# Late constants, larger first pieces, key rotations on GpSimd and reordered seams in a two-layer decoder block

## The chip, the cores and the metric

The kernel runs on one core of a Trainium2 chip. The metric is the device time of one execution in microseconds; of several executions the median is given. A core has a matrix engine (TensorE, "PE" in the profile, with its weight loads as "PEld"), a vector engine (VectorE, "DVE"), a scalar engine (ScalarE, "ACT"), GpSimd ("POOL") and SyncE ("SP"), which here issues most transfers. Each engine works through its own instructions in order and waits on semaphores for the others. Operands lie in SBUF; matmul results lie in PSUM banks.

## What is computed

The input is `x` of 2 x 512 x 1024 and a context `ctx` of 2 x 1024 x 1024, in float32. Four blocks follow each other, each added to `x`:

```python
x = x + matmul(fake_quant(layernorm(x)), fake_quant(ctx))       # quantized product, "layer 0"
x = x + linear_with_routed_lora(layernorm(x))                   # 1024 x 1024, 8 experts of rank 16
x = x + attention(layernorm(x), ctx, ctx, wq, wk, wv, wo)       # 32 query heads, 8 key/value heads, rotary
x = x + linear(layernorm(x)) + gated_lora(layernorm(x))         # 1024 x 1024, the best of 4 experts of rank 8
```

Keys and values depend on the context alone; rotary embedding multiplies keys and queries by a cosine and adds their swapped halves times a sine. The softmax subtracts the row maximum, and its denominators divide the result.

## The kernel before

Nearly every large product is done as a 2x2 block product with seven block products instead of eight (the Strassen-Winograd form). `left_steps` and `right_steps` (L242, L256) form the four extra operands of each side with additions. `seven` (L270) issues the products in the order 1, 2, 6, 7, 5, 4, 3 and hands the four result blocks to `emit`. After product 1 ScalarE copies the accumulator out of PSUM (L284); after the others VectorE adds it (L288, L291, L293, L297, L300). A product of four f32 matmuls of 128x128 by 128x512 (L355, each two instructions of some 0.43 us start to start) takes 3.43 us. `seven_onto` (L304, with the copy at L320 and the addition at L328) does the same onto rows of `x`. Results go to four PSUM buffers of the tag `b` and two of `wide`; SBUF buffers come from the rings `u2`, `u4` and `u8`.

PE's instructions run in the order in which they are written, throughout. In the first stage the orders of DVE and ACT are also written by hand, in the attention loop those of DVE, ACT and POOL. Elsewhere a scheduler orders these engines and the issue queues.

The stages, with their place in the trace: the keys of batch 0 in two halves of weights (q = 0 and 1, held in the list `first`), to about 110 us; the values of batch 0, to 230; the keys and values of batch 1, to 460; the linear block with its LoRA, then the queries, to about 930; attention, to 2300; the last block, to 2448. While PE works at keys and values, the quantized product of layer 0 is woven in (`weave`, L343: one stretch of the side work after every second product).

The first stage loads its weights (`wk_raw`) on SP and its context (`ctx_raw`) mostly on ACT's queue, the first block of each in four pieces. Eight small constants (the quantizer's scales and zero points, router and expert biases, the router matrix, the gate matrix) are loaded on POOL's queue, and DVE works out five values from them ahead of everything. `keys` (L482) rotates each block with `rope` (L208): two swapped-half copies on ACT (L216, L217), then a cosine multiplication (L219), a sine multiplication (L222) and an addition (L223) on DVE. Then SP stores the block (L494). The value weights are loaded by `quad_weights` (L364, loads at L370) after the weave of keys(0, 1), and DVE forms their sums.

`queries` (L668) does the same as the keys for the 32 query heads, eight at a time for the two batches. The last pair (q = 7) runs inside the first attention iterations, with sines on POOL.

`attention` (L856) is a loop over 64 heads (2 batches x 32), with three heads in flight: scores of head n+2 (L768, evicted by DVE with the mask at L782), exponentials of head n+1 (DVE subtracts the maximum at L814, ACT does the exponential at L817, POOL and DVE sum at L820 to L825) and the weighted values of head n (L831). Row maxima and denominators are turned into rows with transposes (L732), a reduction (L734) and two small DMAs through DRAM (`to_row` with L741, `from_row` with L747). Each finished head is divided by its denominators on POOL (`normalize`, L842). Iterations n = -2 and -1 fill the loop; the table `extra` says how many query products are issued within each of the first iterations. Work for the last block hangs on some iterations by `hooks`; `gated` (L956) makes the gate in stretches: matmuls (L967), copies on ACT (L975), then transposes (L981) and a chain of small DVE operations (L982 to L996) that choose the expert.

Of the kernel before, what the change touches and what calls it, by code (L numbers as in the profile page):

```python
# [39 lines left out]
def decoder_kernel(  # L40
# [75 lines left out]
    qp = {}  # L116
    for name, ap in qparams.items():
        t = const.tile([P, 1], F32, name=f"qp_{name}")
        nc.gpsimd.dma_start(t, ap.partition_broadcast(P))
        qp[name] = t  # L120
    for side in ("x1", "x2"):
        t = const.tile([P, 1], F32, name=f"qp_inv_{side}")
        nc.vector.reciprocal(t, qp[f"{side}_scale"])
        qp[f"{side}_inv"] = t

    c_x1 = const.tile([P, 1], F32, name="c_x1")
    c_x2 = const.tile([P, 1], F32, name="c_x2")
    for c_t, side in ((c_x1, "x1"), (c_x2, "x2")):
        nc.vector.tensor_scalar(c_t, qp[f"{side}_zp"], -1.0, QMID, ALU.mult, ALU.add)
    kc2 = const.tile([P, 1], F32, name="kc2")  # L130
    nc.vector.tensor_scalar_mul(kc2, c_x2, float(D))
    s12 = const.tile([P, 1], F32, name="s12")
    nc.vector.tensor_tensor(s12, qp["x1_scale"], qp["x2_scale"], ALU.mult)
    ident_b = const.tile([P, P], BF16, name="ident_b")
# [3 lines left out]
    rb_t = const.tile([P, E0], F32, name="rb_t")  # L138
    nc.gpsimd.dma_start(rb_t, rb0.partition_broadcast(P))
    eb_t = const.tile([P, E1], F32, name="eb_t")  # L140
    nc.gpsimd.dma_start(eb_t, ebias.partition_broadcast(P))
    r0_t = const.tile([P, NC, E0], F32, name="r0_t")
    nc.gpsimd.dma_start(r0_t, r0T.rearrange("(c p) e -> p c e", p=P))
    NGA = E1 + E1 * R1
    ga_t = const.tile([P, NC, NGA], F32, name="ga_t")
    nc.gpsimd.dma_start(ga_t, gaT.rearrange("(c p) e -> p c e", p=P))
    cos_t = [const.tile([P, HALF], F32, name="cos_t"), None]
# [59 lines left out]

    def rope(dst, acc, half, scale):  # L208

        for _ in rope_steps(dst, acc, half, scale, nc.vector):  # L210
            pass
# [57 lines left out]

    def seven(product, emit):  # L270

        banks = {}
        for i in (1, 2, 6, 7, 5, 4, 3):
            first = {2: 1, 4: 7, 3: 5}.get(i, i)
            if i == first:
                banks[i] = ps_b()
            acc = banks[first]  # L280
            product(i, acc, i == first)
            if i == 1:
                u, c22, c21 = u2([P, HALF]), None, None
                nc.scalar.copy(u, acc)  # L284
            elif i == 2:
                emit(0, 0, acc)
            elif i == 6:
                nc.vector.tensor_tensor(u, u, acc, ALU.add)  # L288
            elif i == 7:
                c22 = u2([P, HALF])  # L290
                nc.vector.tensor_tensor(c22, u, acc, ALU.add)  # L291
            elif i == 5:
                nc.vector.tensor_tensor(c22, c22, acc, ALU.add)  # L293
                emit(1, 1, c22)
            elif i == 4:
                c21 = u2([P, HALF])
                nc.vector.tensor_tensor(c21, u, acc, ALU.add)  # L297
                emit(1, 0, c21)
            else:
                nc.vector.tensor_tensor(u, u, acc, ALU.add)  # L300
                emit(0, 1, u)
            yield
# [61 lines left out]
    def quad_weights(dram, q):  # L364

        raw = []
        for mh in range(2):
            for ch in range(2):
                w = u4([P, 4, 256])
                nc.sync.dma_start(w, dram[q, mh, ch])  # L370
                raw.append(w)
        return quad_sums(raw)

# [107 lines left out]

    def keys(b, q, ctx_ops, w):  # L482
        def group(m):
# [7 lines left out]
            def emit(i, j, src):  # L491
                dst = u2([P, HALF]) if (i, j) == (0, 0) else src
                rope(dst, src, j, 1.0)
                nc.sync.dma_start(kT_d[b][4 * q + 2 * i + m][:, ts(j, HALF)], dst)  # L494

            return seven(product, emit)

# [169 lines left out]

    def queries(q, h_ops, w, later=None):  # L668

        def head(m):  # L670
# [7 lines left out]
            def finish(i, j, src):  # L678
                dst = u2([P, HALF]) if (i, j) == (0, 0) else src
                eng = nc.vector if later is None else nc.gpsimd  # L680
                yield from rope_steps(dst, src, 0, ATT_SCALE, eng)
# [174 lines left out]
    def attention(extra):  # L856
# [28 lines left out]
        for n in range(-2, total + GRP + 1):  # L885
# [33 lines left out]
            if n > GRP and gg + 1 < B * NKV:  # L919
                for i in {2: (1, 6, 2), 3: (7, 5, 4, 3)}.get(k, ()):  # L920
                    w_ops[i] = output_operand((gg + 1) % NKV, i)
            for _ in range(extra.pop(n, 0)):
                for _ in range(2):
                    next(tree, None)
                next(extra["products"])
            if n == GRP:
                w_ops = {i: output_operand(0, i) for i in (1, 6, 2, 7, 5, 4, 3)}
# [3 lines left out]

            if mid:
                mid.place_maximum()
# [5 lines left out]
            if old:  # L939
                old.attend(0)  # L940
            if mid:
                mid.exponential(0)
            if old:
                old.den = from_row(old.den)
                if new:
                    new.turn_maximum()
            if mid:
                mid.exponential(1)
            if new:
# [92 lines left out]

    for c in range(4):
        cs = slice(c, c + 1)
        nc.sync.dma_start(wk_raw[0][0][:, cs, :], wk[0, 0, 0][:, cs, :])
# [15 lines left out]
    for ch in range(2):  # L1061
        load_weight(1, 1, ch)


    ctx_ops = [ctx_raw[0], ctx_raw[2]] + [None] * 5
    w = [wk_raw[q][0:2] + [None] * 5 for q in range(2)]
    first = [keys(0, q, ctx_ops, w[q]) for q in range(2)]

# [7 lines left out]
    with tc.manual_schedule(engines={mybir.EngineType.DVE, mybir.EngineType.Activation}):  # L1076
        rights = right_steps(nc.vector, *ctx_raw, lambda: u8([P, 4, HALF]))
        lefts = left_steps(nc.vector, *wk_raw[0], lambda: u4([P, 4, 256]))
        advance(rights, 2)
        advance(lefts, 2)  # L1080
        for g in first[0]:
            next(g)
# [15 lines left out]
        load_rows(0, nc.scalar)  # L1098

    side = layer_0()  # L1100
    for b in range(B):
# [5 lines left out]
        for i, stage in enumerate((keys, keys, values, values)):  # L1107
# [6 lines left out]
            if (b, i) == (0, 1):  # L1114
                main = chain(*first[1])
            else:
                main = pair(*stage(b, i % 2, ctx_ops, w))
            weave(main, side, 2)
            if i < 3:
                w = quad_weights((wk, wv)[(i + 1) // 2], (i + 1) % 2)  # L1120
            if i == 1 and b == 1:
# [42 lines left out]
    h_ops = [hb[0][0], hb[0][1]] + [None] * 5  # L1164
    early = [head for q in range(2) for head in queries(q, h_ops, w[q])]
    for _ in range(2):
# [8 lines left out]
    for q in range(NH // 4):  # L1175
        heads = (
            early[2 * q : 2 * q + 2]
            if q < 2
            else queries(q, h_ops, w, later if q == NH // 4 - 1 else None)
        )  # L1180
        main = chain(*heads) if q < 2 else pair(*heads)
        for g in ((0,), (1,), (2,), (3,), (4,), (5,), (6, 7), ())[q]:
            output_sums(g)
        if q < NH // 4 - 1:
            for _ in main:
                pass
            if q > 0:
# [3 lines left out]

    extra = {-2: 3, -1: 3, 0: 2, 1: 2, 2: 2, 3: 1, 4: 1}
    steps = attention({**extra, "products": main, "later": later})
# [39 lines left out]
    for i in range(2):  # L1233
# [10 lines left out]
    ]  # L1244
    hooks[(62, 1)] = [lambda: advance(last["gates"], 3)]
    hooks[(62, 2)] = [
        lambda: fetch_weight(7, 0, 1),
        lambda: fetch_weight(3, 1, 1),
# [146 lines left out]
```

## Time and profile before

| | us |
|---|---|
| median of 3 runs | 2449.82 (2448.38 to 2452.53) |
| the profiled execution | 2450.07 |
| its span in the profile | 2448.3 |
| PE busy | 2412.5 |
| DVE busy | 1841.1 |
| ACT busy | 530.8 |
| POOL busy | 1031.3 |

The mean granted clock of TensorE was 0.999. By stage, from the trace (busy us of each engine):

| stretch | PE | DVE | ACT | POOL |
|---|---|---|---|---|
| 4 to 110, keys of batch 0 | 102.31 | 74.13 | 21.43 | 2.93 |
| 114 to 230, values of batch 0 | 113.88 | 77.96 | 13.59 | 0.00 |
| 230 to 350, keys of batch 1 | 118.03 | 94.72 | 27.41 | 11.36 |
| 350 to 460, values of batch 1 | 110.00 | 51.61 | 13.46 | 4.02 |
| 930 to 980, seam to attention | 44.99 | 34.41 | 10.37 | 12.12 |
| 980 to 2300, attention | 1312.23 | 1148.65 | 341.71 | 935.85 |
| 2300 to 2448, last block | 143.72 | 71.61 | 9.67 | 40.48 |

A row of the profile reads: start, duration, engine, line of the kernel, operation, output<-input with shapes, count, and in brackets the idle time before it with what ended that wait. A row of waits gives the total, the count and the longest. Matmuls are pipelined, so small sums of busy time say less than the starts do. The loads of the first 35 us moved 9.63 MB.

### The profile page before, as it was taken

How to read it: one execution, taken by the hardware profiler on the slowest of the kernel's cores; microseconds unless marked ns; L12 is line 12 of the kernel's file. 1: busy time of each engine (PE TensorE's matmuls, PEld its weight loads, DVE VectorE, ACT ScalarE, POOL GpSimd, SP SyncE). 2: the span in 40 equal slices, each digit the busy share in tenths (PEclk: the TensorE clock that was granted, in tenths of full speed). 3: DMA queues.
4: the chain of work that ended last, by engine and by line, in shares of the span. 5: the costliest groups of instructions: out<-in, count | busy, mean ns of one | idle time of the engine just before them, and what ended most of it. 6: DMA issues, size and time to landing. Idle time of an engine off the chain costs nothing.

```text
span 2448.3 us, 19583 instructions
## 1 busy us (share of the span) xinstructions
PE 2412.5 (99%) x6792; PEld 1195.8 (49%) x6800; DVE 1841.1 (75%) x1994; ACT 530.8 (22%) x623; POOL 1031.3 (42%) x550
## 2 busy tenths in 40 slices
PE   8999999999999999999999999999999999999999
PEld 3477458654444443444444444444444444444444
DVE  4949774345876556898888888888898998888653
ACT  1210221011222222322222222222222222222210
POOL 0000010210000001677676767667776767677621
PEclk9999999999999999999999999999999999999999
DMA  5537133013796221244323323442433343233501
GB/s 182 181 105 273 69 134 108 26 60 116 274 330 216 78 91 56 77 156 111 81 83 107 114 65 90 142 145 79 125 116 79 94 125 112 66 90 108 172 9 60
DMA packets 149010, 288.01 MB, mean 118 GB/s; under 512 B 29424, under 2 KB 47360, under 8 KB 146608
## 3 DMA queue, kind: packets, MB, share of 16 engines
q1 hardware_dynamic: 108080, 244.35, 29.9%
q10 hardware_dynamic: 40400, 41.70, 6.9%
q8 instruction: 54, 0.88, 0.2%
q0 software_dynamic: 432, 0.71, 0.1%
q14 instruction: 44, 0.36, 0.1%
HBM read 223.54 MB, written 63.18 MB: 117 GB/s over the span
## 4 chain that ended last, share of the span: by engine, by line
PE 60%; DVE 6%; POOL 2%; issue 1%; DMA 1%; ACT 1%; ACTq 0%; SPq 0%; DVEq 0%; POOLq 0%
PE b L355 26%; PE wide L768 16%; PE b L831 15%; PE wide L732 2%; DVE u L814 2%; DMA u<-in_wo_dram 1%; DVE u L782 1%; POOL u L823 0%; POOL u L824 0%; DVE small L734 0%; DVE u L792 0%; DVE u L794 0%; ACT u L817 0%; POOL u L825 0%; DVE u L328 0%
## 5 line engine op out<-in xcount | busy, mean ns | idle before, releaser
L355 PE MATMUL b<-u,u 128*128 128x512 f32 (+1 forms) x3616 | 1394.2, 542 | 21.3 <-DMA u<-in_ctxT_in_dram 7.6
L355 PEld LDWEIGHTS b<-u,u 128*128 128x128 f32 x3616 | 684.6, 191 | 695.9 <-issue 612.8
L768 PE MATMUL wide<-u,u 128*128 128x512 f32 x1024 | 454.8, 595 | 7.3 <-DVE u L782 6.4
L831 PE MATMUL b<-u,u 128*128 128x512 f32 x1024 | 460.3, 592 | 0.0
L782 DVE TENSOR_TENSOR u<-wide,u 128x1024 f32<-128x1024 f32 x256 | 312.8, 1224 | 130.3 <-PE wide L768 129.9
L817 ACT ACTIVATE u<-u 128x2048 f32<-128x2048 f32 x128 | 244.7, 1912 | 655.8 <-DVE u L814 593.9
L768 PEld LDWEIGHTS wide<-u,u 128*128 128x128 f32 x1024 | 193.4, 190 | 257.3 <-issue 177.9
L814 DVE TENSOR_TENSOR u<-u,b 128x2048 f32<-128x2048 f32 x128 | 290.2, 2268 | 0.0
L820 POOL TENSOR_TENSOR u<-u 128x1024 f32<-128x1024 f32 x64 | 151.5, 2367 | 317.5 <-ACT u L817 310.1
L831 PEld LDWEIGHTS b<-u,u 128*128 128x128 f32 x1024 | 186.2, 192 | 184.6 <-issue 184.6
L310 POOL TENSOR_TENSOR u<-u,u 128x512 f32<-128x512 f32 x120 | 188.5, 1597 | 175.4 <-DVE u L322 153.2
L328 DVE TENSOR_TENSOR u<-u,b 128x512 f32<-128x512 f32 x200 | 135.8, 680 | 126.0 <-PE b L355 125.9
L222 POOL TENSOR_TENSOR u<-u,sin_t 128x512 f32<-128x512 f32 x8 | 11.6, 1456 | 402.7 <-ACT u L217 402.7
L823 POOL TENSOR_TENSOR u<-u,u 128x1024 f32<-128x1024 f32 x64 | 150.7, 2354 | 36.4 <-ACT u L817 36.0
L824 POOL TENSOR_TENSOR u<-u,u 128x1024 f32<-128x1024 f32 x64 | 150.8, 2356 | 5.0
L842 POOL TENSOR_TENSOR u<-u,u 128x512 f32<-128x512 f32 x64 | 119.9, 1873 | 10.0 <-DMA u<-row 10.0
L216 ACT ACTIVATE u<-u 64x512 f32<-64x512 f32 x72 | 45.2, 628 | 356.3 <-DVE u L293 177.6
L790 DVE TENSOR_TENSOR u<-u 128x1024 f32<-128x1024 f32 x64 | 115.8, 1810 | 0.0
L732 PEld LDWEIGHTS wide<-ident,u 128*128 128x128 f32 x512 | 79.6, 203 | 63.9 <-issue 55.0
L612 POOL TENSOR_TENSOR u<-u,u 128x1024 f32<-128x1024 f32 x8 | 20.2, 2529 | 214.9 <-DVE u L168 111.6
L792 DVE TENSOR_TENSOR u<-u,u 128x1024 f32<-128x1024 f32 x64 | 105.4, 1646 | 0.2
L825 POOL TENSOR_TENSOR u<-u 128x512 f32<-128x512 f32 x64 | 101.0, 1578 | 5.0
(135 smaller groups left out, 1614.3 us busy)
## 6 DMA issues: line engine op xcount, KB each, us to landing
u<-row ACTq DMA_DIRECT2D x128, 256.0 KB, 3.7
u<-wo SPq DMA_DIRECT2D x64, 512.0 KB, 4.0
u<-in_wo_dram SPq DMA_DIRECT2D x48, 512.0 KB, 4.5
u<-in_wq_dram SPq DMA_DIRECT2D x32, 512.0 KB, 4.2
q<-u SPq DMA_DIRECT2D x64, 256.0 KB, 2.4
u<-in_wo_dram SPq DMA_DIRECT2D x16, 1024.0 KB, 8.2
wo<-u SPq DMA_DIRECT2D x32, 512.0 KB, 4.2
u<-q SPq DMA_DIRECT2D x64, 256.0 KB, 4.2
```

Source lines behind the costliest of these rows:

```text
L310: nc.gpsimd.tensor_tensor(c, c, what, ALU.add)
L328: nc.vector.tensor_tensor(c, c, acc, ALU.add)
L355: nc.tensor.matmul(acc, lhsT, rhs, start=start and k == 0, stop=k == len(pairs) - 1, skip_group_check=True,)
L732: nc.tensor.transpose(tr[:, t, :], src[:, t, :], ident)
L768: nc.tensor.matmul(sc[:, ts(n, HALF)], self.kT[:, ts(2 * j + n, P)], self.qT, start=True, stop=True,)
L782: nc.vector.tensor_tensor(self.e[j // 2][:, js, :], sc.rearrange("p (k q) -> p k q", k=2), mask[j], ALU.add)
L814: nc.vector.tensor_tensor(e, e, self.nmf.unsqueeze(1).to_broadcast([P, 4, S]), ALU.add)
L817: nc.scalar.activation(e, e, AF.Exp)
L820: nc.gpsimd.tensor_tensor(d, e[:, 0:2, :], e[:, 2:4, :], ALU.add)
L823: nc.gpsimd.tensor_tensor(d, d, e[:, 0:2, :], ALU.add)
L824: nc.gpsimd.tensor_tensor(d, d, e[:, 2:4, :], ALU.add)
L831: nc.tensor.matmul(self.acc, self.v[:, k, :], self.e[j][:, k % 4, :], start=(k == 0), stop=(k == NKT - 1),)
```

## The change

Six places are edited.

1. The eight constants are loaded on SP after all other loads of the first stage, and the five values that DVE makes of them are formed after that stage's products in the program's text. The first weight and context blocks come in three pieces, the third of double size. Twenty matmuls of bf16 ones are issued first, into a buffer of the first product. The first product of the first two groups is issued piece by piece, each piece to both groups, and `seven` takes it as `begun`.
2. The value weights' loads are issued before the weave of keys(0, 1); only their sums follow it.
3. `keys` takes an engine for the sine multiplication and the addition, and its queue for the store. The first call keeps VectorE and SP. The other three use GpSimd for the operations and GpSimd's queue for the stores.
4. `queries` is told its engine. The rotations of q = 6 are, like those of q = 7, finished one step later (on VectorE). `extra` becomes 2 and 4 for the iterations -2 and -1. In iteration -1 the maximum and the exponentials of head 0 are placed among the query products.
5. In the steady loop the denominators' load of a head follows the second exponential of the next head instead of standing between the two.
6. At the end one step of `gated` (its transposes and DVE chain) moves from phase 1 to phase 2 of iteration 62.

```diff
-    for name, ap in qparams.items():
-        t = const.tile([P, 1], F32, name=f"qp_{name}")
-        nc.gpsimd.dma_start(t, ap.partition_broadcast(P))
...
-    nc.gpsimd.dma_start(ga_t, gaT.rearrange("(c p) e -> p c e", p=P))
...
-    def seven(product, emit):
+    def seven(product, emit, begun=None):
...
-                banks[i] = ps_b()
+                banks[i] = begun if begun is not None and i == 1 else ps_b()
             acc = banks[first]
-            product(i, acc, i == first)
+            if begun is None or i > 1:
+                product(i, acc, i == first)
...
-    def keys(b, q, ctx_ops, w):
+    def keys(b, q, ctx_ops, w, begun=(None, None), eng=nc.gpsimd):
+
+        queue = nc.sync if eng is nc.vector else eng
...
-                rope(dst, src, j, 1.0)
-                nc.sync.dma_start(kT_d[b][4 * q + 2 * i + m][:, ts(j, HALF)], dst)
+                rope(dst, src, j, 1.0, eng)
+                queue.dma_start(kT_d[b][4 * q + 2 * i + m][:, ts(j, HALF)], dst)
...
-    def queries(q, h_ops, w, later=None):
+    def queries(q, h_ops, w, eng, later=None):
...
-            for _ in range(extra.pop(n, 0)):
+            for i in range(extra.pop(n, 0)):
                 for _ in range(2):
                     next(tree, None)
                 next(extra["products"])
+
+                if mid and not old and i == 1:
+                    mid.place_maximum()
+                    mid.exponential(0)
+                if mid and not old and i == 2:
+                    mid.exponential(1)
...
-            if mid:
+            if mid and old:
                 mid.place_maximum()
...
-            if mid:
-                mid.exponential(0)
-            if old:
-                old.den = from_row(old.den)
+                if mid:
+                    mid.exponential(0)
                 if new:
                     new.turn_maximum()
-            if mid:
-                mid.exponential(1)
+                if mid:
+                    mid.exponential(1)
+                old.den = from_row(old.den)
...
-    for c in range(4):
-        cs = slice(c, c + 1)
+
+    for c in range(3):
+        cs = slice(c, c + 1 + c // 2)
...
+    for name, ap in qparams.items():
+        nc.sync.dma_start(qp[name], ap.partition_broadcast(P))
...
+    begun = [ps_b() for _ in range(2)]
+
+    for i in range(20):
+        nc.tensor.matmul(begun[0][:, :P], ones_b, ones_b, start=True, stop=True)
+    first = [keys(0, 0, ctx_ops, w[0], begun, nc.vector), keys(0, 1, ctx_ops, w[1])]
...
+        for c in range(4):
+            for m in range(2):
+                nc.tensor.matmul(
+                    begun[m],
+                    wk_raw[0][0][:, c, ts(m, P)],
+                    ctx_raw[0][:, c, :],
+                    start=(c == 0),
+                    stop=(c == 3),
+                )
...
+                raw = raw_weights(wv, 0)
+                weave(main, side, 2)
+                w = quad_sums(raw)
...
+            last_two = q >= NH // 4 - 2
+            heads = queries(
+                q, h_ops, w, (nc.vector, nc.gpsimd)[q == NH // 4 - 1], later if last_two else None
+            )
...
+            for i, _ in enumerate(main):
+
+                if i < 13:
+                    for rotation in later:
+                        next(rotation, None)
+                    later.clear()
...
-    extra = {-2: 3, -1: 3, 0: 2, 1: 2, 2: 2, 3: 1, 4: 1}
+    extra = {-2: 2, -1: 4, 0: 2, 1: 2, 2: 2, 3: 1, 4: 1}
...
-    hooks[(62, 1)] = [lambda: advance(last["gates"], 3)]
+    hooks[(62, 1)] = [lambda: advance(last["gates"], 2)]
     hooks[(62, 2)] = [
+        lambda: next(last["gates"]),
         lambda: fetch_weight(7, 0, 1),
```

## The prediction

> **What bounds it.** The page first. TensorE (PE) is busy nearly all the time, so only its stalls and stretches at half clock can be won.
>
> ```profile
> PE 2412.5 (99%) x6792; PEld 1195.8 (49%) x6800; DVE 1841.1 (75%) x1994; ACT 530.8 (22%) x623; POOL 1031.3 (42%) x550
> ...
> L222 POOL TENSOR_TENSOR u<-u,sin_t 128x512 f32<-128x512 f32 x8 | 11.6, 1456 | 402.7 <-ACT u L217 402.7
> ...
> L790 DVE TENSOR_TENSOR u<-u 128x1024 f32<-128x1024 f32 x64 | 115.8, 1810 | 0.0
> ```
>
> Idle PE is 2448.3 - 2412.5 = 35.8 us; the two lower rows price GpSimd (POOL) further down. PE's waits say where it lies:
>
> ```profile
> PE b L355 <- DMA u<-in_ctxT_in_dram: 7.6, 4, 3.9
> PE wide L768 <- DVE u L782: 6.4, 6, 3.6
> PE b L355 <- DMA u<-in_wv_dram: 4.1, 1, 4.1
> PE b L355 <- DVE u L291: 2.9, 3, 1.8
> PE b L355 <- ACT u L320: 2.5, 1, 2.5
> PE b L355 <- ACT u L284: 1.8, 2, 1.6
> ```
>
> These six make 25.3 us (total, times, longest). The change goes to the place of nearly every one. Timelines of each place follow. The start:
>
> ```profile
> 3.88 2.08 PE L355 MATMUL b<-u,u 128*128 128x512 f32 x2 [3.88 <-DMA u<-in_ctxT_in_dram]
> ...
> 13.74 7.58 PE L355 MATMUL b<-u,u 128*128 128x512 f32 x11 [1.24 <-DMA u<-in_ctxT_in_dram]
> ```
>
> PE waits for each context piece and runs steadily from 13.74 only. Its clock record is half until 18.99. The end of keys(0), where the value weights are late:
>
> ```profile
> 110.38 0.42 SPq L370 DMA_DIRECT2D u<-in_wv_dram  x1
> ...
> 113.76 0.32 SPq L494 DMA_DIRECT2D kT<-u  x1
> 114.17 1.35 SPq L370 DMA_DIRECT2D u<-in_wv_dram  x3
> 114.26 1.95 PEld L355 LDWEIGHTS b<-u,u 128*128 128x128 f32 x6 [4.93 <-DMA u<-in_wv_dram]
> ```
>
> The loads stand behind key stores on SP's queue. The seam from queries to attention:
>
> ```profile
> 968.53 4.47 DVE L814 TENSOR_TENSOR u<-u,b 128x2048 f32<-128x2048 f32 x2
> ...
> 972.92 2.35 DVE L782 TENSOR_TENSOR u<-wide,u 128x1024 f32<-128x1024 f32 x2
> ...
> 974.19 2.44 PE L768 MATMUL wide<-u,u 128*128 128x512 f32 x3 [3.60 <-DVE u L782]
> ```
>
> Two exponential inputs (L814) stand ahead of the score evictions (L782) that PE waits for. The last head:
>
> ```profile
> 2283.99 0.68 DVE L734 TENSOR_REDUCE small<-wide 128x4 f32<-128x512 f32 x1
> ...
> 2284.80 4.45 DVE L814 TENSOR_TENSOR u<-u,b 128x2048 f32<-128x2048 f32 x2
> ...
> 2292.70 0.59 ACT L320 COPY u<-b 128x512 f32<-128x512 f32 x1
> ```
>
> The gate's vector operations (2280.12 to 2284.0) hold L734 and L814 back, the exponentials (L817) follow, and the PSUM copy L320 that PE needs comes behind them.
>
> **Part 1, the start.** Pool's eight constant loads leave; their packets run in the 16 DMA engines at 8 to 14 us; from 4 to 14 us these carried 180 to 300 GB/s (some 235 in the mean) against about 395 afterwards. They take about 24 engine-us, 24/16 = 1.5 us of all engines: the context's second half, landed at 28.8, can come 1.5 us sooner at least. The upper bound is 4 us (10 us x 160 GB/s = 1.6 MB of shortfall, at 395 GB/s). I take 3, since part of the shortfall is latency of the small first pieces. Three pieces in place of four also leave the first eight hardware loads free of waits for earlier ones (before, context piece 3 was issued at 3.86, when piece 0 landed). The first products of both groups need 2 x 4 x 0.857 = 6.9 us at full clock and now follow each piece as it lands. With the last piece at about 10 (8 to 12) they end near 13.4 instead of 20.9. That 7.5 is not all kept: products 6 and 7 need sums of context that landed at 24.8 and 28.8, product 5 a bank that DVE's rope leaves at 44.7 for a use at 48.4 (3.7 us of slack, of which the moved reciprocals of the constants eat 0.9). At an unchanged DMA tail 2.8 us are kept; with the tail 3 us sooner 2.8 + 3 = 5.8. Bounds 3 and 7.
>
> Here a rule bears on the size. The Trainium skill, "TensorE: Matmul & The Clock Gate", Part 1: The HAM clock gate, says that the clock doubles after about 3.4 us of sustained work and falls after an idle window as long. The trace has the 3.4 (two half-clock records of 3.413 us, after gaps of 4.1 and 3.6 us); in the start it has a lift 5.25 us after the steady run began. By the rule the twenty warm-up matmuls and work without holes from about 1 us lift it by 7 to 10. By the row's 5.25, counted from the last piece, it would be 15, and the first products would end near 17: still before the tail decides, so both give 5.8. The trace has no bf16 matmul. Its f32 transposes of 128x128 (L732) take 0.16, so the twenty take under 20 x 0.32 = 6.4 us at half clock; above nothing, as they fill an empty stretch. I take 2 to 3 us; at 6.4 the first products still end by 17.
>
> **Part 2, value weights before the weave.** The four wv loads go on SP at about 57 to 71 us, 40 us ahead of use: 4.1 goes, and with it the half clock behind the gap (1.7 us over pace). ACT's copy L284 now comes before the transposes' copy: 1.6 of the next stall goes. Sum 7.4. What is late next is DVE: from 74.6 it has 33.5 us of work before the wv sums are needed at 109, about 1 us to spare; eight context loads queue behind wv on SP, some 6 us later, with use far off. The lower bound is 3 for this part, if DVE is 4.4 late.
>
> **Part 3, sines, adds and key stores on Pool.** Three of the four keys stages move, 24 pieces, each two Pool operations (1.46 + 1.34) and a store issue (0.55 to 0.9): 3.4 to 3.7 us, 14 in a group of 24 us, so Pool holds. DVE loses 24 x 1.39 = 33 us, SP 24 stores. The 1.8 us stall on L291 goes (a 2.84 us add stood ahead of it). Pool's wide layer-0 adds (2.4 to 2.9) interleave with it.
>
> The rule against this: the Trainium skill, "SBUF — State Buffer", Who interferes with whom, says that a DVE instruction with two SBUF inputs and a GpSimd one that reads SBUF share a port pair as a lock; the second to come blocks until the first is done. The rows: L790 takes 1.22 us where no Pool instruction overlaps, 1.83 beside one; L222 on Pool 1.27 alone, 1.46 in the mean. By the rows 16 Pool operations in keys(0, second q) cost DVE at most 16 x 0.6 = 10, about 4 as only part meets such an instruction, against 11 saved there. By the rule it is 0.65 to 1.27 each, 10 to 20, and DVE would be up to 9 us late in part 2's place. I take the rows, and charge 1.5 us of new waits. In keys(1) DVE is busy 95 of 120 us, so either price is covered.
>
> **Part 4, the seam.** Two products instead of three ahead of iteration -1 and four in it, ropes of q = 6 one step later, head 0's exponentials between the products, q loads before q stores. Before: 0.63 + 1.40 + 3.60 + 1.7 (half clock) = 7.3 over pace. Following PE, DVE and ACT through the new order with the measured durations leaves small stalls of 0.1 + 0.45 + 0.45, and one new one: a product's bank waits for DVE's L288, which stands behind an L814, whose input waits for ACT's copy (L810), and that stands behind two rope pairs. It is about 1.9 (2.27 of L814 and 0.68 of L288, less some 1 us that PE has queued). 7.3 - 2.9 = 4.4; bounds 2.5 and 7. PE's longest gap there falls below the 3.4 after which the clock fell, so the 1.7 is in the gain.
>
> **Part 5, denominators.** In 64 heads the load of the denominator row is issued after the second exponential instead of between the two, 1.9 us later (L817 takes 1.91). It is used some 7.5 us later in the trace, so 4 or more are left: 0. Without that cover each 0.1 us costs 64 x 0.1 = 6.4.
>
> **Part 6, gating.** The gate's transposes go behind the last head's sums and attend: L734 and L814 run 4 to 5 us sooner. 2.48 + 0.48 = 3.0 goes. The gate's 3.9 us of DVE work then ends about 2291.0 for a use at 2291.7. Bounds 1.5 and 3.3.
>
> **Sum.** 5.8 + 7.4 + 1.8 + 4.4 + 3.0 = 22.4. New waits: 1.5 (part 3) and 1.0 (a layer-0 row's statistics now early in DVE's order, for rows that arrive at 72 to 78). 22.4 - 2.5 = 19.9. The profiled execution took 2450.07 (span 2448.3 and 1.8 around it), 0.25 over the median 2449.82. 2450.07 - 19.9 - 0.25 = 2429.9.
>
> **Rivals.** *A, DVE late and the DMA tail fixed.* The lock works as the rule has it and the start keeps only 2.8: 22.4 - 3.0 - 6 (a half of DVE's 9 to 12, the rest in slack) - 2.5 = 10.9, 2439. For it: 1 us of spare in part 2. Against: the rows. *B, the stalls move.* Every place is fed by the next product's operands, and PE's gap only goes to the next wait (seam 4.4, start 5.8, wv 7.4 all lost): 22.4 - 17.6 - 2.5 = 2.3, 2447.5, no change. Against: the chains are worked with their slack. *C, slower: the denominators.* If the normalization (L842 on Pool, which the page already shows waiting 10.0 us for a row) comes late enough to hold back Pool's in-order queue and with it the running sums behind it, every head pays. It decides from (19.9 + 4.9)/64 = 0.39 us a head; at half the 1.9, 64 x 0.95 = 61 - 20 gives 2491. Against: 4 us of slack in the worked order.
>
> **Numbers.** Forecast (2422 to 2437) 0.60; A (2437 to 2444) 0.25; B 0.06; C 0.09. 0.2% is 4.9 us, about what a measurement of this kernel can tell from no change. Faster 0.85, same 0.06, slower 0.09. The range 2422 to 2443 holds forecast and most of A, about 0.82.
>
> **What would show it.** Right: PE steady from about 4 us with one early clock lift; no half-clock record near 114 and 974; no wait on in_wv, on L291 for 1.8 us, or on L320 at the end; one L288 wait of about 2 us at the seam; L842's wait still near 10 us. Wrong: DVE's two-input rows above 1.8 us in the keys stages with PE waiting for wv sums at 109; L842 or L732 waiting per head; a start that ends its second products no earlier than before.

## The result, and the profile after

The changed kernel takes 2454.94 us (median of 19 runs, 2452.89 to 2457.73) against 2450.24 (19 runs, 2446.93 to 2454.92) of the kernel before: a ratio of 1.0016, 95% interval 1.0010 to 1.0023. It is slower by 0.16%, where 2429.9, a gain of 20 us, was forecast. The profiled execution took 2454.07 us; its span is 2452.3, 4.0 longer than before.

The lines of the changed kernel have other numbers: L355 is now L343, L284 L272, L291 L279, L293 L281, L219/L222/L223 L205/L208/L209, L494 L488, L612 L606, L782 L775, L814 L807, L768 L761. The constant loads and the formation of their values are at L1063 to L1124.

The view of PE's waits, of the changed kernel (total, times, longest, in us):

```profile
PE b L343 <- DVE u L279: 9.4, 4, 5.1
PE b L343 <- ACT u L272: 5.7, 1, 5.7
PE b L343 <- DVE u L281: 3.5, 1, 3.5
PE b L1003 <- DVE u L994: 3.4, 1, 3.4
PE wide L761 <- DVE u L775: 1.6, 4, 0.6
...
PE b L343 <- DVE u L276: 1.3, 1, 1.3
```

The waits for the value weights and the 3.6 us for L782's successor L775 are gone, and of the context's 7.6 us 0.6 is left, as intended. Five new ones stand in their place: 5.1 and 2.9 us for L279, 5.7 for L272, 3.5 for L281 and 3.4 for L994. All are on VectorE, or on a ScalarE copy (L272) that stands behind work which waits for VectorE.

Both traces hold the same 5824 records of f32 matmuls of 256 or 512 columns, in nearly the same order. So the k-th of them can be laid beside the k-th, and the difference of their starts tells at each place what has been won or lost so far. This table is worked out from the traces (us, changed minus before; negative is ahead; called the offset below). The last four columns are experiments told below. Each column is one execution, whose end can lie some us from the median of its kernel.

| at (us, before) | changed | u_sines | u_wv | stores | best2 |
|---|---|---|---|---|---|
| 30 | -8.15 | -6.92 | -7.17 | -7.30 | -6.90 |
| 78 | -6.97 | -6.37 | -6.66 | -6.92 | -6.89 |
| 95 | -0.16 | -1.02 | -6.66 | -6.92 | -6.89 |
| 109 | +4.63 | +1.30 | +0.11 | -6.92 | -6.90 |
| 120 | -1.43 | -4.76 | -5.94 | -12.98 | -12.95 |
| 140 | +5.30 | -0.54 | -5.94 | -7.58 | -9.22 |
| 341 | +5.30 | -0.54 | -5.94 | -7.57 | -9.22 |
| 360 | +11.39 | -0.64 | -0.95 | -7.56 | -9.05 |
| 928 | +10.23 | -2.24 | -1.49 | -8.15 | -9.62 |
| 980 | +5.24 | -7.22 | -6.54 | -13.15 | -14.62 |
| 2270 | +3.71 | -8.83 | -7.31 | -15.05 | -16.47 |
| 2440 | +3.64 | -8.90 | -5.91 | -12.36 | -17.46 |

The start won 8.15, the value weights 6.06 (109 to 120), the seam 4.99 (928 to 980). Losses: 6.8 from 78 to 95, 4.8 to 109, 6.7 from 120 to 140, 6.1 from 341 to 360. Each is a stall of PE and a stretch at half clock behind it ("half clock": the profile's record of the granted clock is 0.5). The granted clock fell to 0.81 in 82 to 100 us, 0.89 in 100 to 115, 0.86 in 115 to 140 and 0.80 in 345 to 362. Before, it was 1.00, 0.99, 0.94 and 1.00 there.

The start, PE in the timeline of the changed kernel:

```profile
1.06 2.32 PE L1076 MATMUL b<-ones_b 128*128 128x128 bf16 x20 [1.06 <-DVE ones_b L127]
3.96 8.70 PE L1093 MATMUL b<-u,u 128*128 128x512 f32 x16 [0.58 <-DMA u<-in_ctxT_in_dram]
12.49 8.83 PE L343 MATMUL b<-u,u 128*128 128x512 f32 x20
```

There is no hole after 3.96: the first products of both groups end at 12.5. The next view is of the first loss, VectorE and PE at 77 to 87 us:

```profile
77.27 0.69 DVE L149 BATCH_NORM_STATS2 small<-u 128x6 f32<-128x512 f32 x1 [2.04 <-DMA u<-in_x_in_dram]
...
79.99 0.81 DVE L180 TENSOR_SCALAR u<-u,qp_x_inv,qp_x_zp 128x1024 f32<-128x1024 f32 x1 [1.44 <-DMA u<-in_ctx_in_dram]
...
84.60 0.81 DVE L180 TENSOR_SCALAR u<-u,qp_x_inv,qp_x_zp 128x1024 f32<-128x1024 f32 x1 [1.88 <-DMA u<-in_ctx_in_dram]
85.33 0.68 DVE L281 TENSOR_TENSOR u<-u,b 128x512 f32<-128x512 f32 x1
...
86.07 10.19 PE L343 MATMUL b<-u,u 128*128 128x512 f32 x16 [3.47 <-DVE u L281]
```

No GpSimd instruction runs here yet. VectorE waits three times (5.4 us in all) for rows of `x` and `ctx`. The addition L281, for which PE waits, stands behind the last of these in VectorE's order. The trace shows why the rows are late. SyncE issues the first `ctx` row at 72.20, after the last value weight (71.72), and the second at 75.67, behind a key store that waited for VectorE. The next ones go out at 76.17, 77.30 and 80.02, each just as an earlier transfer has landed (76.15, 77.24, 79.96). Before, these loads were issued from 64 us on. The fourth loss, at 347 us, is another thing:

```profile
340.23 8.06 DVE L154 TENSOR_SCALAR u<-u,small,small 128x1024 f32<-128x1024 f32 x1
340.65 2.36 POOL L606 TENSOR_TENSOR u<-u,u 128x1024 f32<-128x1024 f32 x1
...
342.95 1.27 POOL L208 TENSOR_TENSOR u<-u,sin_t 128x512 f32<-128x512 f32 x1
344.18 2.34 POOL L606 TENSOR_TENSOR u<-u,u 128x1024 f32<-128x1024 f32 x1
346.48 1.25 POOL L209 TENSOR_TENSOR u<-u,u 128x512 f32<-128x512 f32 x1
348.21 0.67 DVE L288 TENSOR_TENSOR u<-u,b 128x512 f32<-128x512 f32 x1
...
352.81 2.07 PE L343 MATMUL b<-u,u 128*128 128x512 f32 x2 [5.08 <-DVE u L279]
```

One scaling (L154), 0.81 us alone, stands for 8.06 us (8.06 to 8.08 in u_wv, u_gate and gate_split too). Beside it lie four GpSimd instructions with hardly a pause, two of them the sine and the addition that were moved. It ends 0.56 us after the last of them. L288, L276 and L279 are behind it on VectorE, and PE is behind L279.

### The profile page after: what moved, and what is told of

The parts are those of the page before. It is cut to its first block, busy times and chain, and to the rows that moved or that the text cites. A ratio compares the mean times of both kernels' runs of the same rounds, so it can differ in the third digit from the quotient of the medians.

```text
span 2452.3 us, 19637 instructions
## 1 busy us (share of the span) xinstructions
PE 2416.2 (99%) x6820; PEld 1200.2 (49%) x6820; DVE 1837.1 (75%) x1946; ACT 526.8 (21%) x623; POOL 1114.5 (45%) x614
## 4 chain that ended last, share of the span: by engine, by line
PE 54%; DVE 5%; issue 1%; POOL 0%; ACT 0%; DVEq 0%; POOLq 0%; ACTq 0%
PE b L343 19%; PE wide L761 16%; PE b L824 16%; PE wide L725 2%; DVE u L807 1%; DVE u L787 0%; DVE u L785 0%; DVE u L316 0%; DVE small L727 0%; DVE u L775 0%; PE b L965 0%; PE wide L190 0%; DVE u L789 0%; DVE small L149 0%; POOL u L817 0%
## 5 line engine op out<-in xcount | busy, mean ns | idle before, releaser
L343 PE MATMUL b<-u,u 128*128 128x512 f32 (+1 forms) x3600 | 1390.3, 543 | 22.2 <-DVE u L279 9.4
L343 PEld LDWEIGHTS b<-u,u 128*128 128x128 f32 x3600 | 683.5, 191 | 694.2 <-issue 608.6
L761 PE MATMUL wide<-u,u 128*128 128x512 f32 x1024 | 452.6, 593 | 2.5 <-DVE u L775 1.6
L775 DVE TENSOR_TENSOR u<-wide,u 128x1024 f32<-128x1024 f32 x256 | 313.0, 1224 | 125.2 <-PE wide L761 125.0
L761 PEld LDWEIGHTS wide<-u,u 128*128 128x128 f32 x1024 | 192.8, 190 | 251.0 <-issue 175.3
L807 DVE TENSOR_TENSOR u<-u,b 128x2048 f32<-128x2048 f32 x128 | 290.2, 2268 | 3.0 <-ACT b L803 3.0
L816 POOL TENSOR_TENSOR u<-u,u 128x1024 f32<-128x1024 f32 x64 | 150.7, 2354 | 30.8 <-ACT u L810 30.5
L817 POOL TENSOR_TENSOR u<-u,u 128x1024 f32<-128x1024 f32 x64 | 150.7, 2355 | 5.0
L835 POOL TENSOR_TENSOR u<-u,u 128x512 f32<-128x512 f32 x64 | 115.5, 1804 | 17.1 <-DMA u<-row 17.1
L785 DVE TENSOR_TENSOR u<-u,u 128x1024 f32<-128x1024 f32 x64 | 107.3, 1676 | 0.2
L787 DVE TENSOR_TENSOR u<-u,u 128x1024 f32<-128x1024 f32 x64 | 95.5, 1492 | 0.1
L727 DVE TENSOR_REDUCE small<-wide 128x4 f32<-128x512 f32 x128 | 87.2, 681 | 7.0 <-PE wide L725 7.0
```

The lines of the kernel that those rows point to most:

```text
L343: nc.tensor.matmul(acc, lhsT, rhs, start=start and k == 0, stop=k == len(pairs) - 1, skip_group_check=True,)
L761: nc.tensor.matmul(sc[:, ts(n, HALF)], self.kT[:, ts(2 * j + n, P)], self.qT, start=True, stop=True,)
L775: nc.vector.tensor_tensor(self.e[j // 2][:, js, :], sc.rearrange("p (k q) -> p k q", k=2), mask[j], ALU.add)
L807: nc.vector.tensor_tensor(e, e, self.nmf.unsqueeze(1).to_broadcast([P, 4, S]), ALU.add)
L816: nc.gpsimd.tensor_tensor(d, d, e[:, 0:2, :], ALU.add)
L817: nc.gpsimd.tensor_tensor(d, d, e[:, 2:4, :], ALU.add)
```

## The experiments

Two theories came out of these views. The **port theory**: VectorE is held while GpSimd computes, and the moved sines and additions did that. The **queue theory**: the value weights ahead of the context rows made VectorE late at 82, and the later stalls are the same lateness again. Thirteen kernels tell them apart. Ratios are to the kernel before on the same chip, with 95% intervals.

**u_sines**, part 3 undone:

```diff
-    def keys(b, q, ctx_ops, w, begun=(None, None), eng=nc.gpsimd):
+    def keys(b, q, ctx_ops, w, begun=(None, None), eng=nc.vector):
```

> The changed kernel with the keys' sines, additions and stores of the three later key halves back on VectorE and SyncE (part 3 undone, the rest kept). Port theory (VectorE instructions are held for whole GpSimd instructions): the stalls at 102.5 (3.1 us) and 347 (5.1 us) and most of that at 125 (5.9 us) go, with the half-clock stretches behind them; the 1.8 us stall near 342 of the kernel before returns; net about -14, 2441. Queue theory (the value weights ahead of the context rows' loads make VectorE late, and that lateness is what shows again at 102 and 125): only the stall at 347 goes, net about -5, 2450. In both the stall at 82 stays at about 3.5 us.

Measured: 2443.08, 0.9976 (0.9967 to 0.9984), 0.40% under the changed kernel's ratio. PE's idle time at 347 fell from 5.1 to 1.7 us, without a half-clock stretch, that at 102 from 2.9 to 1.0, that at 125 from 5.7 to 4.1. The one at 82 stayed at 3.4. So both theories hold a part. By the table the two kernels differ by 2.5 + 2.5 + 6.2 = 11 us (95 to 109, 120 to 140, 341 to 360). That is what part 3 costs beside part 2; it is not all hold, since in this run 4.1 us at 125 are left with no GpSimd instruction near, and VectorE's instructions there take their lone times. The copy L272 for which PE waits stands in ScalarE's order behind the layer norms' L161, which waits for VectorE's statistics.

**u_wv**, part 2 undone:

```diff
-                raw = raw_weights(wv, 0)
-                weave(main, side, 2)
-                w = quad_sums(raw)
+                weave(main, side, 2)
+                w = quad_weights(wv, 0)
```

> The changed kernel with the value weights loaded after the weave again (part 2 undone, the rest kept). Queue theory: the stall at 82 (3.6 us and 3.4 at half clock) goes and with it those at 102 and 125; the wait for the value weights (4.1 and 1.7) and the 1.6 behind it return; net about -9, 2446. Port theory: 82 goes, 102 stays near 3 us as GpSimd still holds VectorE, and the wait for the value weights returns; net about 0, 2455.

Measured: 2443.22, 0.9972 (0.9964 to 0.9981). The stall at 82 is gone whole, with its half clock: 6.8 us. The one at 102 is not (3.5 us idle, with half clock 6.8), as the port theory has it. The one at 125 shrinks to the 1.6 us of before, although the sines are still on GpSimd. What neither expected: no wait for the value weights came back. With the key stores on GpSimd's queue, SyncE has nothing in front of these loads, so the early issue was not needed.

**u_gate**, part 6 undone:

```diff
-    hooks[(62, 1)] = [lambda: advance(last["gates"], 2)]
+    hooks[(62, 1)] = [lambda: advance(last["gates"], 3)]
...
-        lambda: next(last["gates"]),
```

> The changed kernel with the gate's transposes ahead of the last head again (part 6 undone). Both theories: the 3.4 us wait for L994 goes, and the 2.5 and 0.5 of the kernel before return; net -0.5 (between -1 and 0). If the port is what made the gate's small operations slow (5.5 us beside GpSimd in place of 3.0), they take 3.9 us in all again, since no sum of the last head runs on GpSimd then.

Measured: 2452.51, 1.0013 (1.0006 to 1.0019). The intervals of this and the changed kernel overlap; by the trace 1.0 us is won between 2270 and 2440, none in the changed kernel. L984, L989 and L994 take 0.73, 0.98 and 0.90 here. In the changed kernel they lie beside GpSimd's sums of the last head:

```profile
2290.53 2.35 POOL L816 TENSOR_TENSOR u<-u,u 128x1024 f32<-128x1024 f32 x1
...
2290.98 1.93 DVE L984 TENSOR_TENSOR small<-u,eb_t 128x16 f32<-128x16 f32 x1
...
2292.95 2.34 POOL L817 TENSOR_TENSOR u<-u,u 128x1024 f32<-128x1024 f32 x1
2293.15 2.18 DVE L989 TENSOR_TENSOR small<-small,small 128x16 f32<-128x16 f32 x1
...
2296.80 1.84 DVE L994 TENSOR_TENSOR u<-u,small 128x128 f32<-128x128 f32 x4
...
2298.79 0.63 PE L1003 MATMUL b<-ident,u 128*128 128x128 f32 x4 [3.37 <-DVE u L994]
```

Two operations on 16 elements a partition (L984, L989) take 2 us each: each begins while a GpSimd instruction runs and ends just after it.

**u_adds**, the first linear block's bias additions on VectorE:

```diff
-            nc.gpsimd.tensor_tensor(rows(b, t), rows(b, t), b_t, ALU.add)
+            nc.vector.tensor_tensor(rows(b, t), rows(b, t), b_t, ALU.add)
```

> The changed kernel with the eight additions of the first linear block's bias (L606, 128x1024) on VectorE in place of GpSimd. Port theory: in keys(1) the one scaling that took 8.06 us (L154) falls to under 3, the stall at 347 falls from 5.1 to under 2, net -5 to -7, 2449. Rival (VectorE simply has too much to do there): the additions are 8 x 1.2 = 9.8 us more of VectorE's work, four of them in that stretch, and the stall grows to 6 or more, net 0 or later.

Measured: 2449.84, 1.0005 (0.9996 to 1.0014). The stall at 347 fell from 5.1 to 2.35 us, and L154 there takes 0.8 to 1.4 (1.4 is the mean of two). VectorE has more to do in this run and is earlier: it was not short of time but held.

**stores**, the keys' arithmetic on VectorE throughout, all key stores on GpSimd's queue, value weights after the weave (u_sines and u_wv together, and):

```diff
-        queue = nc.sync if eng is nc.vector else eng
+        queue = nc.gpsimd
```

> The changed kernel with all sines and additions of the keys on VectorE, all key stores on GpSimd's queue, and the value weights loaded after the weave. It separates the stores' move from the arithmetic's. Port theory with the queue theory: SyncE's queue is free, so the value weights arrive in time although they are asked for late, the context rows are not held back, and no GpSimd arithmetic holds VectorE: no stall at 82, at 102 nor for the value weights, only the 1.8 us near 342 returns; at 140 us of the kernel before the offset is -10 to -12 us, the whole about -16, 2433. If instead VectorE was late at 102 for another reason than the port, about 3.5 us and its half clock stay: 2439.

Measured: 2435.79, 0.9936 (0.9919 to 0.9953), faster than both kernels. No stall over 0.6 us from 4 to 109. The two undone parts nearly add up: 0.40% and 0.44% alone, 0.80% together. The arithmetic's move alone, this run against u_wv, is 0.36%. At 140 us the offset is -7.6, where -10 to -12 was expected: it is -13 at 120, and then a product waits 3.45 us for the copy L272. ScalarE's order has the layer norms' L161 ahead of it, which waits for VectorE's statistics. It is of the kind of the 1.6 us for L284 of before, which is there as well.

**gate_split**, the gate's transposes early, its VectorE chain late:

```diff
             nc.tensor.transpose(tr[:, t, :], sums[:, ts(t, P)], ident)
+        yield
```

> The changed kernel in which the gate's transposes stay ahead of the last head, while its VectorE chain comes behind that head's exponential inputs. Port theory: the chain starts about 2 us earlier, at 2288.3 in place of 2290.3 of the changed kernel, mostly before GpSimd's sums begin, takes 4 us in place of 8.3, and the 3.4 us wait for L994 shrinks to under 1: net -3. If the small operations are slow for another reason, the chain keeps its 8 us and the wait shrinks by 2 only.

Measured: 2456.56, 1.0025 (1.0016 to 1.0035). The miss is of the order, not of the hold: the chain did start at 2288.6, but GpSimd's first sum had started at 2288.5. It is held from its third operation on, and takes 10.3 us from start to end instead of 8.3; PE waits 3.65.

**halves**, each GpSimd sine and addition cut in two:

```diff
+        pieces = [slice(0, HALF)] if eng is nc.vector else [slice(0, 256), slice(256, HALF)]
+        for c in pieces:
+            eng.tensor_tensor(rot[:, c], rot[:, c], sin_t[half][:, c], ALU.mult)
```

> The changed kernel with each of GpSimd's sine multiplications and additions cut into two of 128x256. If VectorE is held for one GpSimd instruction at a time, single holds fall from about 1.1 us to 0.6 and the stalls at 102 and 347 shrink by a third or more: net -3. If it is held until GpSimd pauses, whatever the number of its instructions (one scaling stood 8.06 us beside four of them in a row), the stalls stay or grow by the extra instructions: net 0 to +4.

Measured: 2456.89, 1.0018 (1.0008 to 1.0028). The stall at 347 grew from 5.1 to 6.8 us. The timeline there:

```profile
344.19 9.84 DVE L205 SCALAR_TENSOR_TENSOR u<-u,u 128x512 f32<-128x512 f32 x1 [1.42 <-ACT u L203]
344.84 1.40 POOL L210 TENSOR_TENSOR u<-u,sin_t 128x256 f32<-128x256 f32 x2
346.20 1.39 POOL L212 TENSOR_TENSOR u<-u,u 128x256 f32<-128x256 f32 x2
...
352.74 1.86 POOL L210 TENSOR_TENSOR u<-u,u 128x256 f32<-128x256 f32 x2
```

Both cases occur. From 89 to 99 us most single holds do fall: scalings and products that took 1.75 us in the changed kernel take 1.21 (0.69 to 0.81 alone), and GpSimd's halves take longer, so the two engines take turns. But where GpSimd's instructions follow each other with no gap, VectorE can be held through the run: here one L205, 0.69 alone, for 9.84 us. It ends 0.56 us after the first half of the last pair shown, in which GpSimd did not pause. What decides between a turn and a run is not shown.

**wv_pool**, u_sines with the early value weights on GpSimd's queue:

```diff
-                raw = raw_weights(wv, 0)
+                raw = raw_weights(wv, 0, nc.gpsimd)
```

> The changed kernel with the keys' sines and stores back on VectorE and SyncE, and the early loads of the value weights on GpSimd's queue, idle there. If the stall at 82 comes from SyncE's queue order and its waits for landed transfers, it goes and the whole is about -8 against the run with only part 3 undone: 2435. If it comes from the transfers' share of the DMA engines, it stays: 2443.

Measured: 2445.99, 0.9977 (0.9969 to 0.9985). No stall at 82: it was SyncE's order. But the whole is no better. The scheduler put two of the four loads at 1.6 and 2.3 us on the empty queue. They share the DMA engines with the first context pieces (the third lands at 13.6 us, 8.9 in the changed kernel), and the start's gain falls from 7 to 1.7 us. And PE still stalls at 102 (2.7 us) and 125 (6.0 us), which costs 3.9 and 6.8 by the offsets, as much as in the changed kernel. Here no GpSimd arithmetic runs, VectorE's instructions take their lone times, and no row is late at 82. It works from 94.7 to 108 us without a pause, with scalings ahead of L279. So with the value weights early, the order given to VectorE and ScalarE is by itself enough for stalls at these two places.

**best2**, stores with the gate in the order of before:

```diff
-    hooks[(62, 1)] = [lambda: advance(last["gates"], 2)]
+    hooks[(62, 1)] = [lambda: advance(last["gates"], 3)]
```

> All key arithmetic on VectorE, all key stores on GpSimd's queue, the value weights loaded after the weave, the gate as in the kernel before; the new start, seam and denominators kept. Both theories: -12.4 of the run with the stores alone, and the end as before (0.5 + 2.5 of waits in place of 3.4 and a half-clock stretch behind it) gives 1 to 3 more: 2432 to 2435.

Measured: 2433.96, 0.9935 (0.9921 to 0.9948), the fastest of all: 15 us under the kernel before. It has one stall over 2 us left, 3.46 for L272 at 110.

**consts_pool**, best2 with the eight constants back on GpSimd's queue at their old place:

```diff
+    for name, ap in qparams.items():
+        nc.gpsimd.dma_start(qp[name], ap.partition_broadcast(P))
+    nc.gpsimd.dma_start(rb_t, rb0.partition_broadcast(P))
...
-    for name, ap in qparams.items():
-        nc.sync.dma_start(qp[name], ap.partition_broadcast(P))
-    nc.sync.dma_start(rb_t, rb0.partition_broadcast(P))
```

> The kernel of the same call with the eight small constants back on GpSimd's queue at the start. It sizes their share of the start's 7 us: if their small packets hold the DMA engines, context piece 3 and the second half land 3 us or more later and half of the 7 is lost, +3; if the gain comes of the larger pieces, the earlier issue and the order by piece, under +1.

Measured: 2440.86, 0.9960 (0.9946 to 0.9974). At 78 us it is 2.25 ahead in place of 6.89, so 4.6 of the start's 6.9 us is the constants' place. The third context piece lands at 11.5 us (8.6 in best2), the last of the first stage's context at 28.7 (23.8). The medians differ by 6.9, more than either expectation. Of the rest, 1.65 us comes at 120 to 140, where this run has a half-clock stretch after a gap of 3.47 us and best2 has none after one of 3.46.

**memset**, GpSimd writes zeros in place of computing:

```diff
-        eng.tensor_tensor(rot, rot, sin_t[half], ALU.mult)
-        eng.tensor_tensor(dst, dst, rot, ALU.add)
+        if eng is nc.gpsimd and scale == 1.0:
+            eng.memset(rot, 0.0)
+            eng.memset(dst[:, 0:1], 0.0)
+            return
```

> The changed kernel in which GpSimd writes zeros over the swapped halves (and one column of the keys) in place of multiplying and adding: the keys' sine part is left out, GpSimd only writes and reads nothing. Port theory: VectorE's cosine multiplications and sums (two operands in SBUF) take 0.69 and 1.22 beside it again, and the stalls at 102 and 347 fall below 2; net -5 to -9. If VectorE is late through the order of instructions and waits for GpSimd's results, both stalls stay near 3 and 5.

Measured: 2435.27, 0.9938 (0.9925 to 0.9952). The stalls at 102, 125 and 347 are gone, the one at 82 stays (3.1). But these writes take 0.52 us each, a third of what they replace. This leaves open whether reading or mere length is what holds, and part of the gain may come of the changed order.

**start_only**, the kernel before with part 1 alone:

```diff
-        nc.gpsimd.dma_start(t, ap.partition_broadcast(P))
...
+        cs = slice(c, c + 1 + c // 2)
...
+        nc.sync.dma_start(qp[name], ap.partition_broadcast(P))
...
+        nc.tensor.matmul(begun[0][:, :P], ones_b, ones_b, start=True, stop=True)
...
+                nc.tensor.matmul(
+                    begun[m],
```

> The kernel before with part 1 of the change alone (late constants on SyncE, larger pieces, first product by pieces, warm-up). The queue theory says that a start earlier by 7 us is kept in full until the value weights, where the wait depends on key stores that move with it: net -6 to -7, 2443. If the later stages are bound by transfers, part of it is given back at 72 to 114 us: net -3.

Measured: 2444.43, 0.9977 (0.9970 to 0.9985). Of the 7.1 us won at 30 us, 6.4 are kept up to the value weights (wait 4.0 there, as before) and beyond: -6.4 at 109, -6.6 at 200, -7.6 at 928. The profiled execution has -9.9 at the end, of which 1.7 comes at the seam, where its stall (3.6) brought no half-clock stretch. It is the fastest of the 17 runs; the medians differ by 4.8.

**memset_long**, as memset, with six writes of the halves for each piece:

```diff
         if eng is nc.gpsimd and scale == 1.0:
-            eng.memset(rot, 0.0)
+            for _ in range(3):
+                eng.memset(rot, 0.0)
             eng.memset(dst[:, 0:1], 0.0)
+            for _ in range(3):
+                eng.memset(rot, 0.0)
             return
```

> The changed kernel in which GpSimd writes zeros six times over the swapped halves (and once over one column of the keys) in place of multiplying and adding, so that it is busy about as long as in the changed kernel (some 3.2 us a piece); the keys' sine part is left out. If what holds VectorE is that GpSimd reads SBUF, VectorE stays at its lone durations in the keys stages, and the stalls at 102 and 347 stay away as with the short writes: about 2435. If any GpSimd work holds it, its instructions lengthen to 1.2 to 1.8 again and the stalls return: 2448 or more.

Measured: 2443.96, 0.9967 (0.9952 to 0.9981). Neither expectation holds whole. The timeline, where the stall at 102 now measures 5.9 (L210 and L213 are the writes, L350 and L286 are L343 and L279 of the changed kernel):

```profile
96.34 0.67 DVE L205 SCALAR_TENSOR_TENSOR u<-u,u 128x512 f32<-128x512 f32 x1
...
96.94 3.87 DVE L183 TENSOR_SCALAR u<-u 128x1024 f32<-128x1024 f32 x1
97.37 0.54 POOL L213 MEMSET u<- 128x512 f32 x1
...
99.70 0.54 POOL L210 MEMSET u<- 128x512 f32 x1
...
105.86 2.07 PE L350 MATMUL b<-u,u 128*128 128x512 f32 x2 [5.88 <-DVE u L286]
```

The instructions with two operands in SBUF keep their lone time beside the writes, wherever they meet in the keys stages: L205 0.67 here, at most 0.69, and VectorE's wide sums at most 1.23. The scalings with one operand in SBUF (L183, 0.69 alone) are held by writes as well, and by a run of six of them: 3.87. At 347 no stall is left, although GpSimd is busy for 19.9 of 20 us there (330 to 350): the scalings that are held there (L154, 2.10 for one and 4.30 for two) end before PE needs what stands behind them. So two kinds of hold act in the changed kernel, one by GpSimd's reads on two-operand instructions, one by any GpSimd work on scalings.

## Why the prediction was wrong

Two steps failed: that the context loads behind the value weights had "use far off", and that GpSimd's arithmetic was priced by two rows of the profile ("I take the rows"). Smaller ones, the gating among them, are named in turn.

**The start** (5.8 forecast): 8.15 at 30 us, 6.97 after a wait of 0.9 for L205 at 40. The clock came as the rule had it, even a little sooner: full from 6.92 us (7 to 10 by the rule, 18.99 before), and the products run without a hole from 3.96. The mis-sized term was the tail: the context's last piece lands 4.8 us sooner, not 3, and the constants' place alone is worth 4.6.

**Value weights** (7.4): the wait and its half clock went (6.06). The failed step is "eight context loads queue behind wv on SP, some 6 us later, with use far off". The use was not far off: VectorE has a scaling of these rows in its order ahead of a sum that PE needs. This cost 6.8 from 78 to 95, as u_wv and wv_pool show, and the 1.6 of L284 did not go but grew to 5.7 (4.1 in u_sines, 1.6 again in u_wv). The forecast followed the move to SyncE's queue, but not on to who waits for the loads that were moved past, and in which order.

**Sines on GpSimd** (1.8 won, 1.5 charged): the other failed step is "I take the rows". The row of L790 is a mean of two-operand instructions beside a part of a GpSimd instruction. It says nothing of scalings, nor of GpSimd instructions in a row. The rule that was weighed against it, the Trainium skill's "SBUF — State Buffer", Who interferes with whom, has both kinds: two-operand instructions against GpSimd's reads, and scalings among the forms that can hold the whole pair. The runs agree with it on which instructions meet (memset_long), and hold VectorE longer than the one instruction it speaks of (8.06 us for 0.81). That the two meet at a port is what the page states; the runs show the hold alone. Rival A had this mechanism and was sized at 6. Moving the arithmetic cost about 10 us of the time with part 2 kept (0.40%) and 9 without (0.36%), since the stalls of the changed kernel in these stages also cost 1.7 to 3.2 us each of half clock. "In keys(1) DVE is busy 95 of 120 us, so either price is covered" failed there most: the mean has room, the chain behind one held instruction has none.

**Seam** (4.4): 4.99, with the small waits 0.59 (a q load), 0.41 (L775) and 1.25 (L276, formerly L288) where about 2.9 were expected. The mechanism and nearly the size were right.

**Denominators** (0): the offset stays at +5.9 from 1100 to 1900 us. L835, formerly L842, waits 17.1 us for rows in place of 10.0 in all, which PE does not feel. Rival C is out. Another 2.1 us came between 1900 and 2100 and was not traced further.

**Gating** (3.0): 0.07. The waits of 2.5 and 0.5 went, but the chain of small operations took 8.3 us in place of 3.9 beside GpSimd's sums. "The gate's 3.9 us of DVE work" was a duration from a place with little GpSimd work, carried to one with much.

**In sum**, 22.4 of gains were forecast. The start, the value weights and the seam brought 6.97 + 6.06 + 4.99 = 18.0. The new waits were put at 2.5 and cost 6.8 + 4.8 + 6.7 + 6.1 = 24.4 (with the waits of before at these places taken off). With -2.8 of smaller ones this makes the +3.6 of the table's last row. Of the four, 6.8 at 82 us goes to part 2 and 6.1 at 347 to part 3, by u_wv and u_sines. The 4.8 at 102 and the 6.7 at 125 are not cleanly divided:

| lost, us | changed | u_sines | u_wv | stores | wv_pool |
|---|---|---|---|---|---|
| 95 to 109 | 4.8 | 2.3 | 6.8 | 0.0 | 3.9 |
| 120 to 140 | 6.7 | 4.2 | 0.0 | 5.4 | 6.8 |

At 102 either part alone brings a loss. At 125 it also depends on the order in which the scheduler puts L161 and L272 on ScalarE, which changes from kernel to kernel and which no run here fixes.

Undoing the two failed parts and the gating, with the stores kept on GpSimd's queue, gives 15 us of the 20 that were forecast.

## What to carry to other kernels

A step that is moved to GpSimd to relieve VectorE must be priced by what VectorE does at that moment: short scalings and two-operand sums can be held through a whole run of GpSimd instructions, however short they are, and cutting GpSimd's instructions in two did not help here. Moving only the key stores' issues there cost nothing visible here and freed SyncE. When loads are brought forward on a queue, look up the first reader of every load that they pass, and what stands behind that reader on its engine. Where a scheduler sets an engine's order, a moved load can also change that order, and with it who waits.

## What the runs showed that was not expected

A VectorE scaling of 0.81 us was held for 8.06 by four GpSimd instructions in a row, one of 0.69 for 3.87 by a run of writes, and a two-operand product of 0.69 for 9.84 by halved instructions. An idle stretch of PE of 2.9 us (3.5 from start to start) at 102 us brought a half-clock stretch of 1.7 us over pace in the changed kernel, though it is shorter than the 3.4 us that the prediction reckoned with, while one of 3.46 at 110 us in best2 brought none (clock 1.00 in 115 to 140 us; 0.94 in stores, whose gap there is 3.45). So the cost of such a gap is not fixed by its length alone. The eight constants, 0.19 MB in all, took 4.6 us from a start that moves 9.63 MB.
